# Half of a graph product with seven block products for eight, in a graph-attention kernel on one core

## The chip, the cores and the metric

The kernel runs on one core of one Trainium2 chip. Its time is the device time of one execution in microseconds. Each number from a trace comes from one profiled execution. Engines are named as the profile names them: PE (TensorE; PEld is its weight load), DVE (VectorE), ACT (ScalarE), POOL (GpSimd) and SP (SyncE, which here only issues transfers).

## The reference, cut to what matters

Two layers work on x of shape (16, 1024, 256): 16 images of 1024 nodes with 256 channels. The change lies in layer 0, in the product of the normed features with a weighted adjacency matrix.

```
h   = max(layernorm(x), 0)
fea = transpose(h, (0, 2, 1))                   # 256 channels x 1024 nodes
c   = mean over channels of fea                 # 1024 per image
A   = |  |sigmoid(c[m] - c[n]) - 0.5| - 0.5 | * 2, made symmetric
Wg  = adj * A                                   # 1024 x 1024 per image
g   = relu((fea @ Wg) * para)                   # the graph product
q   = g as queries, 4 heads of 64;  k, v = h @ kv_w
x   = x + softmax(q k^T * scale) v
# layer 1
h   = max(layernorm(x), 0)
x   = x + batchnorm(relu(batchnorm((A_hat @ h) @ W1^T + b1)) @ W2^T + b2)
```

## The kernel before

Everything is float32. The images run one after another, and the stages of neighbouring images are interleaved. The order of the instructions on PE, ACT, DVE, POOL and SP is the order in which the code records them (a manual schedule); every engine, and the queue of transfers that SP issues, works through its own list in that order. A wait arises where an instruction needs another engine's result, or a buffer that is still being read. Such buffers come from pools with a fixed number of places for each tag (`bufs`).

For image b the main loop records: `attention(b)`, then `graph(b+1)`, then `linear1_all(b)`, the first matmuls of layer 1. Work for image b+2 (norm, sums) is recorded inside linear1.

**graph(b)** multiplies h (8 chunks of 128 nodes, each 256 channels wide) with w (8 chunks of 128 x 1024, called `f_w`). For each chunk c there are four block products of 128x128 by 128x512: two halves of the channels (d) times two halves of the columns (g). They accumulate in two PSUM tiles `f_gps`, of two banks each. A chunk of w is made by `weights(b, c)`: Abs and Tanh on ACT, and on DVE the multiplication with the resident adjacency (the "mask", L350). The w tiles have five places (`w4`), so chunk c+5 is begun when chunk c has been used.

Between the chunks stand other steps (the dictionary `between`):

- `turn_h` turns h (DVE), and POOL issues 32 small transfers that place it as `f_hT` for keys and values.
- `left` holds what attention(b-1) left over: `[add0, collect, invert, spread, scale, add1]`. The attention output of an image comes in two halves g. For each half, `scale` multiplies by the reciprocal sums (L599) and issues 16 transfers on SP (L612) into the tile `f_att`; `add` adds that tile to the residual x (L620). `f_att` comes from the pool `ow` with one place. `add0` belongs to the first half, whose transfers were issued during attention; the other five belong to the second half.
- `norm` is the layer norm ahead of layer 1: `stats`, `invert` (a power on POOL), `shifts` and `relu` (eight activations on ACT).
- At chunk 5 SP loads `para` (two transfers of 512 KB, L387), and at chunk 6 the sums of key weights (`f_kt`, L393).

After the eight chunks, `queries` multiplies PSUM by `para` (L416, DVE) and applies Relu (L417, ACT). `values` makes v with two groups of products (`f_vps`, L424), each copied out by ACT (L431). The keys come from two halves by two blocks with seven products in place of eight (`mult`, L468; the copies on ACT are L478, L483, L488 and L493). One PSUM bank `f_kpsx` is added to several times there and copied out between the additions, so each addition waits for the copy before it. `f_vps`, `f_kpsx` and `f_gps` share three PSUM places of two banks with the score tiles of attention.

**linear1** starts with products of `norm.h` and the normalised adjacency (`f_aps`, L704). Inside it, the statistics of image b+2 run on DVE, and its relus on ACT ahead of the copy L756. Its x is loaded by SP (`arrive`, L189) into the place of the x that `leave` (L944) has just stored.

Of the kernel before, what the change touches and what calls it, by code (L numbers as in the profile page):

```python
# [29 lines left out]
def fast_path(  # L30
# [143 lines left out]
    with ExitStack() as stage:  # L174
# [115 lines left out]
        def prepare_start(b):  # L290

            sums_of[b] = small.tile([P, NC], F32, tag="sums", name=f"f_sums_{b}")
            norms[b] = Norm(xs[b], f"a{b}", sums_of[b])
            norms[b].stats(0, NC)
            norms[b].invert()
# [46 lines left out]
        def weights(b, c):  # L342


            w = w4.tile([P, N], F32, tag="w4", name=f"f_w_{b}_{c}")
            nc.scalar.activation(  # L346
                w, rows[b], AF.Abs, bias=cols[b][:, c : c + 1], scale=0.5 / C
            )
            nc.scalar.activation(w, w, AF.Tanh)  # L349
            nc.vector.scalar_tensor_tensor(w, w, 1.0, adj_t[c], ALU.subtract, ALU.mult)  # L350
            ws[b, c] = w

        hTs = {}

# [20 lines left out]
        def graph(b, between):  # L375


            gps = [ps_s.tile([P, N], F32, tag="s", name=f"f_gps_{b}_{d}") for d in range(CC)]
            hT = None
            para_t = []  # L380
            for c in range(NC):
                for step in between.get(c, ()):
                    step()
                if c == 5:
                    for d in range(CC):
                        t = w4.tile([P, N], F32, tag="w4", name=f"f_para_{b}_{d}")
                        nc.sync.dma_start(t, para_v[:, d, :])  # L387
                        para_t.append(t)
                if c == 6 and b > 1:
                    t23 = pp.tile([P, 2, 512], F32, tag="acc", name=f"f_kt23_{b}", bufs=2)  # L390
                    rest = pp.tile([P, 2, 512], F32, tag="acc", name=f"f_kt4_{b}", bufs=2)
                    sums = rest[:, 1].rearrange("p (n q) -> p n q", n=4)
                    nc.sync.dma_start(sums, kvs_d)  # L393
                w = ws.pop((b, c))
                blocks = [(d, g) for d in range(CC) for g in range(NH)]
                if b == 0 and c == 0:
                    blocks.sort(key=lambda n: n[1])
                for d, g in blocks:
                    nc.tensor.matmul(  # L399
                        gps[d][:, ts(g, 512)],  # L400
                        hs[b][:, c, ts(d, P)],
                        w[:, ts(g, 512)],
                        start=(c == 0),
                        stop=(c == NC - 1),
                    )
                if c == 0:
                    hT = hTs.pop(b)
            for step in between.get(NC, ()):
                step()
            kT = big.tile([P, CC, N], F32, tag="kT", name=f"f_kT_{b}")  # L410
            qT = big.tile([P, CC, N], F32, tag="qT", name=f"f_qT_{b}")
            v = big.tile([P, NC, C], F32, tag="v", name=f"f_v_{b}")

            def queries(d):

                nc.vector.tensor_mul(qT[:, d, :], gps[d], para_t[d])  # L416
                nc.scalar.activation(qT[:, d, :], qT[:, d, :], AF.Relu, scale=-SCALE)  # L417

            def values():
                for c4 in range(0, NC, 4):  # L420
                    ps = ps_s.tile([P, 4, C], F32, tag="s", name=f"f_vps_{b}_{c4}")
                    for i in range(4):
                        for e in range(CC):
                            nc.tensor.matmul(  # L424
                                ps[:, i, :],
                                hT[e][:, ts(c4 + i, P)],
                                kvw_t[:, e, C : 2 * C],
                                start=(e == 0),
                                stop=(e == CC - 1),
                            )  # L430
                    nc.scalar.copy(v[:, c4 : c4 + 4, :], ps)  # L431

            late = between.get("late", ())
            if b < 2:
                for step in late:
                    step()
                for d in range(CC):
                    ps = ps_s.tile([P, N], F32, tag="s", name=f"f_kps_{b}_{d}")
                    for g in range(NH):
                        for e in range(CC):  # L440
                            nc.tensor.matmul(  # L441
                                ps[:, ts(g, 512)],
                                kvw_t[:, e, ts(d, P)],
                                hT[e][:, ts(g, 512)],
                                start=(e == 0),
                                stop=(e == CC - 1),
                            )
                    nc.scalar.copy(kT[:, d, :], ps)
                    queries(d)
                values()  # L450
                return qT, kT, v

            t2, t3, t4 = t23[:, 0], t23[:, 1], rest[:, 0]
            part = lambda k, j: hT[k][:, ts(j, 512)]
            a = lambda i, k: kvw_t[:, k, ts(i, P)]
            for d in range(CC):
                queries(d)
            nc.vector.tensor_sub(t3, part(1, 1), part(0, 1))  # L460
            nc.vector.tensor_add(t2, t3, part(0, 0))
            nc.vector.tensor_sub(t4, part(1, 0), t2)
            values()
            t1 = part(0, 1)
            nc.vector.tensor_sub(t1, t1, part(0, 0))

            def mult(ps, left, right, more=False):
                nc.tensor.matmul(  # L468
                    ps, left, right, start=not more, stop=True, skip_group_check=more
                )  # L470

            c = lambda i, j: kT[:, i, ts(j, 512)]
            x = ps_s.tile([P, 512], F32, tag="s", name=f"f_kpsx_{b}")
            m7 = ps_s.tile([P, 512], F32, tag="s", name=f"f_kps7_{b}")
            m2 = ps_t.tile([P, 512], F32, tag="t", name=f"f_kps2_{b}")
            m4 = ps_o.tile([P, 512], F32, tag="o", name=f"f_kps4_{b}")
            mult(x, a(0, 0), part(0, 0))
            nc.scalar.copy(c(0, 0), x)  # L478
            mult(m2, a(0, 1), part(1, 0))
            nc.vector.tensor_add(c(0, 0), c(0, 0), m2)  # L480
            late[0]()
            mult(x, sums[:, 1], t2, True)
            nc.scalar.copy(c(1, 0), x)  # L483
            late[1]()
            mult(m7, sums[:, 2], t3)
            nc.vector.tensor_add(c(1, 0), c(1, 0), m7)
            mult(x, sums[:, 0], t1, True)
            nc.scalar.copy(c(1, 1), x)  # L488
            mult(m4, a(1, 1), t4)
            nc.vector.tensor_add(c(1, 1), c(1, 1), m7)  # L490
            nc.vector.tensor_add(c(1, 0), c(1, 0), m4)
            mult(x, sums[:, 3], part(1, 1), True)
            nc.scalar.copy(c(0, 1), x)  # L493
            return qT, kT, v

        def attention(b, qT, kT, v, hooks):

# [549 lines left out]
        with tc.manual_schedule(engines={ENG.PE, ENG.Activation, ENG.DVE, ENG.Pool, ENG.SP}):  # L1047
# [73 lines left out]
            for b in range(B):  # L1121
# [35 lines left out]
                if b + 1 < B:  # L1157
                    if 0 < b < B - 2:
                        thirds = load_thirds(b)
                    qkv = graph(b + 1, between)  # L1160
                    if b == 0:
                        for step in scale[4:]:
                            step()
                        thirds = make_thirds(b)
                if b + 2 < B:
# [1 line left out]
                        b,  # L1167
                        norm.h,
                        thirds,
                        lambda: prepare_start(b + 2),  # L1170
                        lambda: prepare_end(b + 2),
                        lambda: (prepare_row(b + 2), again(b + 1)),
                    )
# [55 lines left out]
    with ExitStack() as stage:  # L1229
# [21 lines left out]
        with tc.manual_schedule(engines={ENG.PE, ENG.Activation, ENG.DVE, ENG.Pool, ENG.SP}):  # L1251
# [40 lines left out]
            class Pair:  # L1292
# [49 lines left out]
                def m1(self):  # L1342
                    self.x = bank(f"f_zx_{self.p}", ps_x)
                    self.mult(self.x, a(0, 0), self.b[0, 0], True)

                def m2(self):
                    ps = bank(f"f_zm2_{self.p}")
                    self.mult(ps, a(0, 1), self.b[1, 0], True)
                    self.add(0, 0, ps)

                def m6(self):
                    self.mult(self.x, sums[:, 1], self.t2)
# [5 lines left out]
                def m5(self):  # L1358
                    self.mult(self.x, sums[:, 0], self.t1)

                def m3(self):
                    self.mult(self.x, sums[:, 3], self.b[1, 1])

                def m4(self):
                    self.mult(self.m, a(1, 1), self.t4)
# [20 lines left out]
            def plain(t, ps, f2):  # L1386
                for c in range(CC):
                    product(ps[c], t, c, f2)
# [717 lines left out]
```

## Time and profile before

| | |
|---|---|
| three runs | 2424.45, 2425.27, 2425.93 us; median 2425.27 |
| the profiled execution | 2425.91 us, of which 2424.1 are the span of the trace |
| mean granted TensorE clock | 0.995 |
| PE busy | 2384.8 us, 98% of the span |
| DVE, ACT, POOL busy | 1781.2, 1325.8 and 308.6 us |
| one image in the middle, graph product | 27.57 us (32 block products) |
| the same image, values and keys | 13.67 us |
| the same image, linear1 | 36.14 us |

The page gives busy time by engine, then the span in slices, the queues of transfers, the chain that ended last, and groups of instructions by line. A timeline line gives the start and the length in us, the engine, the line of the code, the operation, the tile written and the tiles read, the shape and the count; in square brackets stands how long the engine had idled before it, and what released it.

### The profile page before, as it was taken

To read this page: it belongs to the slowest core of one execution; us is meant where nothing else is said; L and a number is where in the kernel's file an instruction comes from. 1 tells how busy PE (TensorE), PEld (TensorE's weight loads), DVE (VectorE), ACT (ScalarE), POOL (GpSimd) and SP (SyncE) were. 2 spreads that over 40 slices of the span, in tenths; PEclk is the share of its full clock that TensorE was granted. 3 is DMA by queue.
4 is the path that set the end of the run, shared out by engine and by line. 5 is a ranking of instruction groups with operands and counts; after the bars stand their busy time and mean duration, and the time that the engine had idled before them with its cause. 6 is when DMAs were issued, how large, how long until landed. Compare 5 with 4: busy or idle time off the path is not lost.

```text
span 2424.1 us, 24651 instructions
## 1 busy us (share of the span) xinstructions
PE 2384.8 (98%) x8034; PEld 1050.7 (43%) x8034; DVE 1781.2 (73%) x2442; ACT 1325.8 (55%) x1932; POOL 308.6 (13%) x547
## 2 busy tenths in 40 slices
PE   8999999999999999999999999999999999999995
PEld 4453444434343434444343434344443434444444
DVE  6878778685959586786859595877868596757766
ACT  6845555464646455554646464555546465446654
POOL 2030202021020302020200203020202011000000
PEclk9999999999999999999999999999999999999998
DMA  5041414222332414142323324142423222355569
GB/s 187 9 140 61 152 61 126 87 88 74 115 95 62 146 61 152 61 126 87 89 73 115 95 63 146 61 152 61 126 87 88 73 68 85 101 192 195 176 239 375
DMA packets 176633, 275.76 MB, mean 114 GB/s; under 512 B 37872, under 2 KB 121328, under 8 KB 176496
## 3 DMA queue, kind: packets, MB, share of 16 engines
q1 hardware_dynamic: 156336, 241.55, 30.7%
q0 software_dynamic: 15552, 15.77, 2.5%
q10 hardware_dynamic: 4608, 16.78, 1.7%
q8 instruction: 66, 1.08, 0.2%
q14 instruction: 71, 0.58, 0.1%
HBM read 169.35 MB, written 71.10 MB: 99 GB/s over the span
## 4 chain that ended last, share of the span: by engine, by line
PE 93%; DVE 3%; DMA 2%; issue 1%; SPq 1%; POOL 0%; ACT 0%; DVEq 0%; ACTq 0%; POOLq 0%
PE f_s L507 17%; PE f_o L548 17%; PE f_gps L399 17%; PE f_aps L704 16%; PE f_zps L810 6%; PE f_vps L424 4%; PE f_zx L1326 4%; PE f_zm L1326 3%; PE f_kpsx L468 2%; PE f_kps L468 1%; DVE f_acc L524 1%; PE f_outps L1546 1%; PE f_z2ps L1264 1%; PE f_kps L441 1%; PE f_zps L892 1%
## 5 line engine op out<-in xcount | busy, mean ns | idle before, releaser
L515 ACT ACTIVATE f_p<-f_s 128x1024 f32<-128x1024 f32 x512 | 477.3, 1046 | 151.8 <-PE f_s L507 151.7
L524 DVE TENSOR_TENSOR f_acc<-f_acc,f_p 128x1024 f32<-128x1024 f32 x384 | 470.5, 1225 | 41.1 <-ACT f_p L515 0.5
L507 PE MATMUL f_s<-f_qT,f_kT 64*128 64x512 f32 x2048 | 456.8, 596 | 0.0
L548 PE MATMUL f_o<-f_p,f_v 128*64 128x512 f32 x2048 | 453.6, 595 | 0.0
L399 PE MATMUL f_gps<-f_w,f_h_a 128*128 128x512 f32 x1024 | 444.7, 594 | 0.3 <-DVE f_w L337 0.3
L369 POOL DMA_DIRECT2D f_hT<-f_hQ x480 | 235.9, 499 | 1221.7 <-PE f_gps L399 1170.8
L507 PEld LDWEIGHTS f_s<-f_qT,f_kT 64*128 64x128 f32 x2048 | 190.7, 185 | 263.6 <-ACT f_p L515 117.1
L399 PEld LDWEIGHTS f_gps<-f_w,f_h_a 128*128 128x128 f32 x1024 | 192.8, 190 | 247.0 <-issue 230.0
L548 PEld LDWEIGHTS f_o<-f_p,f_v 128*64 128x64 f32 x2048 | 141.4, 137 | 304.3 <-issue 254.2
L350 DVE SCALAR_TENSOR_TENSOR f_w<-f_w,f_adj 128x1024 f32<-128x1024 f32 x127 | 153.8, 1212 | 39.1 <-ACT f_w L349 39.1
L346 ACT ACTIVATE f_w<-f_row,f_col 128x1024 f32<-128x1024 f32 x127 | 147.0, 1157 | 29.3 <-DMA f_row<-frow 28.5
L279 ACT ACTIVATE f_h_b<-f_x,f_shift_b,f_rstd_b 128x256 f32<-128x256 f32 x128 | 67.9, 594 | 162.5 <-DVE f_shift_b L264 162.5
L349 ACT ACTIVATE f_w<-f_w 128x1024 f32<-128x1024 f32 x127 | 134.3, 1057 | 4.0
L704 PE MATMUL f_aps<-f_ahatT,f_hs 128*128 128x512 f32 x256 | 115.1, 592 | 0.0
L424 PE MATMUL f_vps<-f_kvw,f_hT 128*128 128x256 f32 x512 | 113.4, 379 | 0.2 <-DVE f_qT L416 0.2
L704 PE MATMUL f_aps<-f_ahatT,f_h_b 128*128 128x512 f32 x256 | 112.7, 593 | 0.0
L704 PE MATMUL f_aps<-f_t,f_hs 128*128 128x512 f32 x256 | 112.5, 592 | 0.0
L279 ACT ACTIVATE f_h_a<-f_x,f_shift_a,f_rstd_a 128x256 f32<-128x256 f32 x126 | 73.8, 587 | 62.6 <-DVE f_shift_a L264 62.6
L424 PEld LDWEIGHTS f_vps<-f_kvw,f_hT 128*128 128x128 f32 x512 | 97.2, 190 | 20.6 <-issue 7.4
L521 DVE TENSOR_TENSOR f_acc<-f_p,f_p 128x1024 f32<-128x1024 f32 x64 | 76.2, 1191 | 15.3 <-ACT f_p L515 15.3
L590 ACT COPY f_recs<-f_rec 32x32 f32<-32x32 f32 x128 | 31.5, 246 | 98.7 <-DVE f_rec L582 97.5
L575 ACT COPY f_parts<-f_red 32x64 f32<-32x64 f32 x128 | 39.0, 305 | 78.5 <-DVE f_red L540 77.3
(230 smaller groups left out, 2705.7 us busy)
## 6 DMA issues: line engine op xcount, KB each, us to landing
f_t<-ft SPq DMA_DIRECT2D x84, 512.0 KB, 6.9
fz<-f_z SPq DMA_DIRECT2D x64, 512.0 KB, 9.9
f_x<-in_x_dram SPq DMA_DIRECT2D x31, 1024.0 KB, 5.9
f_zb<-fz SPq DMA_DIRECT2D x42, 512.0 KB, 4.2
f_para<-in_L_gnn_para_dram SPq DMA_DIRECT2D x32, 512.0 KB, 4.5
f_att<-f_oT SPq DMA_DIRECT2D x512, 32.0 KB, 1.9
fx<-f_x SPq DMA_DIRECT2D x16, 1024.0 KB, 6.5
f_hT<-f_hQ POOLq DMA_DIRECT2D x480, 32.0 KB, 2.6
```

The costliest lines, as they stand in the source:

```text
L346: nc.scalar.activation(w, rows[b], AF.Abs, bias=cols[b][:, c : c + 1], scale=0.5 / C)
L350: nc.vector.scalar_tensor_tensor(w, w, 1.0, adj_t[c], ALU.subtract, ALU.mult)
L369: queue.dma_start(to[ts(k, 32), ts(a, 32 * NC)], t[ts(a, 32), k].rearrange("i c r -> i (c r)"),)
L399: nc.tensor.matmul(gps[d][:, ts(g, 512)], hs[b][:, c, ts(d, P)], w[:, ts(g, 512)], start=(c == 0), stop=(c == NC - 1),)
L424: nc.tensor.matmul(ps[:, i, :], hT[e][:, ts(c4 + i, P)], kvw_t[:, e, C : 2 * C], start=(e == 0), stop=(e == CC - 1),)
L507: nc.tensor.matmul(ps[:, e, :], kT[rows_e, pair, ts(m, P)], qT[rows_e, pair, ts(g, 512)], start=True, stop=True,)
L515: nc.scalar.activation(p, ps, AF.Exp)
L524: nc.vector.tensor_add(acc_of[s], acc_of[s], p)
L548: nc.tensor.matmul(o_of[s][e * HD : (e + 1) * HD, :], v[:, m, ts(2 * pair + e, HD)], p[:, e, :], start=(m == 0), stop=(m == NC - 1),)
L704: nc.tensor.matmul(ps, left[:, m, :], right(m), start=not more and m == 0, stop=(m == KH - 1), skip_group_check=more,)
L810: nc.tensor.matmul(ps[i], left[:, ts(i, P)], right, start=not more, stop=True, skip_group_check=more,)
L1326: nc.tensor.matmul(ps, left[:, m, :], right[:, m, :], start=start and m == 0, stop=(m == 1), skip_group_check=not start,)
```

## The change

Images 2 to 15 take a new function `graph_seven`; images 0 and 1 keep `graph`. In it:

- Chunks 0 to 3 are multiplied as before (`plain`). Chunks 4 to 7 form two pairs, (4, 5) and (6, 7). Each pair is a product of two by two blocks with two by two blocks, done with seven block products. All pairs add into the same banks: the two `f_gps` tiles, one bank x and one bank m7.
- That needs sums of h (`s1` to `s4`, 128x256 each) and differences of w (`t1` to `t4`, 128x512 for each pair), all on DVE. `t1` and `t4` are made in place. `t2` and `t3` lie in the tile that later holds the keys.
- x is copied out three times on ACT, into the tile that later holds the values (`room`). DVE then adds m7 and the `f_gps` banks to it, and multiplies the sum by `para`. `para` is loaded in one transfer of 1 MB into the tile of the queries (`f_qT`) and multiplied in place.
- `add0` is recorded behind the seven-product part; `collect`, `invert`, `spread` and `scale` stay between the first chunks; `add1` goes to the keys. The statistics of the norm go behind the queries and into the keys; its relus, the query relus, `leave` and `arrive` are recorded between or behind the key products.

```diff
         def weights(b, c):
+            differences(b, c)
+            masked(b, c)
+
+        def differences(b, c):
             w = w4.tile([P, N], F32, tag="w4", name=f"f_w_{b}_{c}")
...
+            gps = [ps_s.tile([P, N], F32, tag="s", name=f"f_gps_{b}_{d}") for d in range(CC)]
+            add0, collect, invert, spread, scale, add1 = left
...
+            turn_h(b)
+            differences(b, 2)
+            masked(b, 2)
+            collect()
+            invert()
+            differences(b, 3)
+            masked(b, 3)
+            differences(b, 4)
+            spread()
+            scale()
+            masked(b, 4)
+            plain(0)
+            differences(b, 5)
+            masked(b, 5)
...
+            nc.vector.tensor_sub(s3, a(0, 0), a(1, 0))
+            nc.vector.tensor_add(s1, a(1, 0), a(1, 1))
+            nc.vector.tensor_sub(s2, s1, a(0, 0))
+            nc.vector.tensor_sub(s4, a(0, 1), s2)
+            plain(1)
+            differences(b, 6)
+            masked(b, 6)
...
+            make_t3(0)
+            make_t1(0)
+            plain(2)
+            differences(b, 7)
+            masked(b, 7)
+            make_t2(0)
+            plain(3)
+            qT = big.tile([P, CC, N], F32, tag="qT", name=f"f_qT_{b}")
+            nc.sync.dma_start(qT, para_v)
...
+            nc.sync.dma_start(sums, kvs_d)
+            make_t3(1)
+            make_t1(1)
+            make_t2(1)
...
+            m1(0)
+            m2(0)
+            m1(1)
+            nc.scalar.copy(room[:, 0], x)
+            m_7(0)
+            m3(0)
+            m2(1)
+            make_t4(0)
+            make_t4(1)
+            m6(0)
+            m_7(1)
+            m3(1)
+            m6(1)
+            nc.scalar.copy(room[:, 2], x)
+            m4(0)
+            m4(1)
+            m5(0)
+            m5(1)
+            nc.scalar.copy(room[:, 1], x)
+            add0()
+            nc.vector.tensor_add(room[:, 2], room[:, 2], m7)
...
+            nc.vector.tensor_sub(kt3, part(1, 1), part(0, 1))
+            nc.vector.tensor_add(kt2, kt3, part(0, 0))
+            nc.vector.tensor_sub(kt4, part(1, 0), kt2)
+            nc.vector.tensor_add(room[:, 3], room[:, 1], m7)
+            both = lambda d: room[:, 2 * d : 2 * d + 2].rearrange("p n k -> p (n k)")
+            for d in range(CC):
+                nc.vector.tensor_add(both(d), both(d), gps[d])
+            for d in range(CC):
+                nc.vector.tensor_mul(qT[:, d, :], both(d), qT[:, d, :])
...
+            norm.stats(0, 4)
+            norm.invert(0, 4)
+            values(b, hT, v)
...
+            mult(x, aw(0, 0), part(0, 0))
             nc.scalar.copy(c(0, 0), x)
+            mult(k2, aw(0, 1), part(1, 0))
+            nc.vector.tensor_add(c(0, 0), c(0, 0), k2)
+            norm.shifts(0, 4)
+            add1()
+            norm.stats(4, NC)
+            norm.invert(4, NC)
+            leave(b - 1)
+            arrive(b + 1)
+            mult(x, sums[:, 1], kt2, True)
             nc.scalar.copy(c(1, 0), x)
+            behind[0](todo)
...
             nc.scalar.copy(c(1, 1), x)
+            behind[1](todo)
...
             nc.scalar.copy(c(0, 1), x)
+            behind[2](todo)
+            return (qT, kT, v), todo
```

For images 2 to 14 `behind` holds the norm's relus (two chunks, two chunks, four chunks), and the query relus follow in linear1. For image 15 it holds the two query relus and then all eight relus of the norm.

## The prediction

> **What bounds the kernel now.** I read the page's busy line first, then the TensorE timeline of one image in the middle of the run, and then the other engines' timelines over the same stretch.
>
> ```profile
> PE 2384.8 (98%) x8034; PEld 1050.7 (43%) x8034; DVE 1781.2 (73%) x2442; ACT 1325.8 (55%) x1932; POOL 308.6 (13%) x547
> ```
>
> TensorE has 39 us of 2424 free, most of it at the two ends. So removed TensorE work pays in full, and any new stall costs in full. The timeline of image 8 (start and length in us):
>
> ```profile
> 1055.47 27.73 PE L399 MATMUL f_gps<-f_w,f_h_a 128*128 128x512 f32 x64
> 1083.04 3.62 PE L424 MATMUL f_vps<-f_kvw,f_hT 128*128 128x256 f32 x16
> 1086.83 3.72 PE L424 MATMUL f_vps<-f_kvw,f_hT 128*128 128x256 f32 x16 [0.17 <-DVE f_qT L416]
> ...
> 1092.14 1.12 PE L468 MATMUL f_kpsx<-f_kt,f_kt 128*128 128x512 f32 x2
> ...
> 1096.71 7.03 PE L704 MATMUL f_aps<-f_ahatT,f_h_b 128*128 128x512 f32 x16
> ```
>
> Each product of 128x128 by 128x512 is two records. The row's mean of 594 ns is a latency: 64 records fill 1083.04 - 1055.47 = 27.57 us, so one product costs 27.57 / 32 = **0.86 us**. Below, times count from the graph product's start, T = 1055.47. The third key product (`f_kpsx` from `f_kt`) starts at T+36.7, linear1 at T+41.2.
>
> VectorE and SyncE in that stretch:
>
> ```profile
> 1061.18 1.21 DVE L620 TENSOR_TENSOR f_x<-f_x,f_att 128x1024 f32<-128x1024 f32 x1
> ...
> 1064.73 1.21 DVE L599 TENSOR_TENSOR f_oT<-f_oT,f_recs 128x1024 f32<-128x1024 f32 x1
> ```
>
> ```profile
> 1065.96 10.18 SPq L612 DMA_DIRECT2D f_att<-f_oT  x16
> 1076.24 1.00 SPq L387 DMA_DIRECT2D f_para<-in_L_gnn_para_dram  x2
> 1077.55 0.33 SPq L393 DMA_DIRECT2D f_kt<-fkvs  x1
> ```
>
> L620 is the first half's residual add (left[0]); it is the last reader of the only `att` buffer (pool `ow`, bufs=1). It ends before L599 (scale), so the second half's 16 transfers into that buffer start as L599 ends. SyncE spends 10.2 us issuing them, 0.64 each, and only then issues `para` and the key sums, early enough for L416 at T+30.
>
> **What the Trainium skill says.** "DMA: Bandwidth & Descriptors", section "Anatomy of one DMA — SWDGE (gpsimd) path": any semaphore wait happens on the issuing sequencer before dispatch; the DMA engines don't wait. The lines above agree (L612 begins 0.02 us after L599's end): a held transfer holds the queue behind it. "VectorE: DVE Perf Modes", section "The TRN2 errata — SBUF-src ops pay a fixed extra latency per instruction": an fp32 tensor_tensor takes (N+151)/0.96 ns. The page's 690 ns at 512 and 1225 at 1024 agree; 128x256, which this trace lacks, is then an estimated 0.42 us. "TensorE: Matmul & The Clock Gate", section "Part 1: The HAM clock gate (the "warmup" mystery)": after an idle window of about 3.4 us the array runs at half clock until a busy window has passed. The kernel's tail agrees, in the timeline and in the windows (columns: window, length, busy PE, PEld, DVE, ACT, POOL, granted clock, DMA share, GB/s):
>
> ```profile
> 2386.90 6.36 PE L1546 MATMUL f_outps<-f_ident,f_z 128*128 128x128 f32 x32 [5.37 <-ACT f_z L1526]
> 2393.69 2.13 PE L1546 MATMUL f_outps<-f_ident,f_z 128*128 128x128 f32 x16 [0.44 <-DVE f_x1t L1587]
> ```
>
> ```profile
> 2385.00:2390.00 5.00, 3.08 (x13) 2.69 (x14) 0.82 (x1) 3.61 (x3) 0.00 (x0) 0.51 1.02 368
> 2390.00:2395.00 5.00, 4.56 (x30) 3.96 (x30) 4.30 (x5) 3.62 (x3) 0.00 (x0) 0.81 1.03 420
> ```
>
> After 5.4 us idle the clock is 0.51, and a 5 us window at mean 0.81 was at half clock for 1.9 us: the gate opened some 5 us after the restart, 2 to 2.5 us of work lost.
>
> **The change, part by part** (images 2 to 15, 14 in all).
>
> TensorE: chunks 4 to 7 take 14 products instead of 16: -2 x 0.86 = -1.72 us an image, -24 us in all. The graph product ends at T+25.8 if its operands are in time.
>
> VectorE operands: `w2`'s mask ends its slot at T+5.7 as before. Then collect's reduction, reciprocal, most and least (1.28), `w3` mask (1.14 start to start): 8.1. Scale waits for spread, which ScalarE reaches after `w4` (7.5, +1.02): it runs 8.5 to 9.6. Masks of `w4` and `w5`: 11.9. Four 128x256 sums of h (0.34 to 0.46 start to start): 13.5. `w6` mask 14.65, t3 and t1 of pair 0: 16.0, `w7` mask 17.1, then six 128x512 differences at 0.60 to 0.72: 21.0. TensorE wants `w7` at T+18, the last t at T+23: **hidden**. If that cover were gone, all 11 us that VectorE gains an image (4 x 0.42 + 10 x 0.69 + 2 x 1.22) would be at stake.
>
> The three ScalarE copies of x (0.59 each) lie behind other products: nothing. The adds of both halves and room before the queries would let the second value product begin at T+30.1, where TensorE arrives at 29.2: 0.9 us, absorbed in what follows.
>
> **add0 moves** behind all of this, to T+21.0, ending at 22.2. Scale's 16 transfers stay ahead of it, but write the one `att` buffer that add0 still has to read. The first must wait for add0: it starts at T+22.2 instead of 10.5. Queued behind on SyncE are 15 more transfers, `para` (now one of 1 MB, into qT), the key sums, the store of x and the load of x of b+2. So:
>
> - 16 issues at 0.64: `para` is issued at T+32.4.
> - It lands 5.4 us later, at 37.8. Bounds: 3.8 (the smallest `f_para`) to 6.5. Two 512 KB ones took 4.5 each, half a us apart; 1 MB of x takes 5.9:
>
> ```profile
> f_x<-in_x_dram SPq DMA_DIRECT2D x31, 1024.0 KB, 5.9
> f_para<-in_L_gnn_para_dram SPq DMA_DIRECT2D x32, 512.0 KB, 4.5
> fx<-f_x SPq DMA_DIRECT2D x16, 1024.0 KB, 6.5
> ```
>
> - The two query multiplications: 1.14 + 1.22, to 40.15.
> - v serves as room that they read, so ScalarE's copies of the value products wait for them: the second is done at 41.2. The first key copy is queued behind: 41.75.
> - The third key product adds into the bank that this copy reads: T+41.8 instead of 36.7, **+5.1 us**.
>
> TensorE has by then been idle from 35.2, 6.6 us: cold clock. Five us at half rate, of which ScalarE's copies between key products hide a little: **+2.3 us** (0 to 3.5). Linear1 starts at T+48.6.
>
> Later norm: add1, stats and inversion (44.6 to 47), shifts and the eight relus of 0.55 fit ahead of linear1's needs chunk by chunk: nothing. The store of x issues at 44.6 instead of 23.8 and lands after 6.5; the next load then takes 5.9, to 57. Linear1's VectorE wants x at 7.7 us after its start, 56.3: 0.7 late, covered by the slack ahead of L753 (2.8 us idle). If it takes longer, up to 1.5 us lands on the product that waits for L756's copy. The query relus move into linear1, where ScalarE idles 6.3 us: nothing.
>
> Image 15: no linear1 follows; eight relus (4.3 us) stand ahead of the first exponentials, and score tiles have three buffers (2.65 us of TensorE work): +3.4 us.
>
> Sum: 14 x (5.1 + 2.3) + 3.4 = 107 us; the 1.72 saved are already inside, since both times are absolute. The profiled execution took 2425.9 us (span 2424.1 and 1.8 around it), so 2533; the median is 0.6 lower: **2532 us**.
>
> **The rivals.**
> 1. *TensorE's saving decides.* If the transfers were not held (another buffer, or a wait met early), the third key product could start when VectorE's additions allow, about T+35.3 against 36.7: -1.4 x 14 = -20 us, 2405; at best -24, 2401. For it: the product's operands are in time. Against: one `att` buffer. It decides only if `para` lands before about T+32.5, where issue alone takes until 32.4.
> 2. *The late queue also breaks linear1.* The load of x for b+2 slips further and the norm for the next image delays L756's copy: +1.5 us an image, `para` at 6.5 and the cold clock for a second window (+1.2 each): 14 x (7.4 + 3.9) + 3.4 = +162, 2587. For it: nothing on SyncE is late now, but a dozen transfers become so. Against: 2.8 us of slack at L753.
> 3. *The delay without the clock*: the gate stays open and `para` takes 3.8: 14 x 3.5 + 3.4 = +52, 2477. Against: 6.6 us of idle against the tail's 5.4.
>
> **How the numbers follow.** Forecast 0.75, rival 2 0.13, rival 3 0.09, rival 1 0.03. The range 2488 to 2575 holds the first with its bounds and about half of rivals 2 and 3. About 0.2% (5 us) is what a measurement can tell from no change; only rival 1 is faster: 0.03, within it 0.01, slower 0.96.
>
> **What would show it.** In the changed profile the second `f_att` group should begin only when the first `f_x<-f_x,f_att` add of the image ends; `f_kpsx` should wait about 6.6 us on ScalarE's `f_kT` 14 times; the granted clock should sink to about half for some 5 us in each keys stage; DVE busy should be near 1935 us, PE records 56 fewer. It is wrong if `para` is issued before T+28, if the keys stage has no gap, or if the wait stands in the graph product itself (VectorE late), where I put none.

## The result: slower by 4.3%, and the profile after

The changed kernel takes 2529.28 us (median; 2527.63 to 2531.64) against 2425.6 for the kernel before beside it: ratio 1.0428, 95% interval 1.041 to 1.0447. The forecast was 2532. The profiled spans are 2525.8 and 2424.1, so there are 101.7 us to account for. One run each of two kernels further down took 4190 and 9855 us; it counts in the median there, but not in the ratio. Times written T+ count, as in the prediction, from the start of an image's graph product.

The page of the changed kernel, the line of busy times:

```profile
PE 2387.9 (95%) x7978; PEld 1050.9 (42%) x7978; DVE 1926.7 (76%) x2694; ACT 1348.1 (53%) x1974; POOL 318.1 (13%) x561
```

The removed products are gone (7978 records against 8034) and VectorE has gained 145 us, yet TensorE's share fell: the span grew, not the work. The list of TensorE's waits names one place (what waited, for what: us in total, times, longest):

```profile
PE f_kpsx L625 <- ACT f_kT L641: 92.3, 14, 7.7
```

TensorE's timeline of image 8, T = 1101.20 (start, length in us, idle before):

```profile
1101.20 14.00 PE L469 MATMUL f_gps<-f_w,f_h_a 128*128 128x512 f32 x32
...
1127.06 3.62 PE L444 MATMUL f_vps<-f_kvw,f_hT 128*128 128x256 f32 x16
1131.94 3.72 PE L444 MATMUL f_vps<-f_kvw,f_hT 128*128 128x256 f32 x16 [1.27 <-DVE f_v L610]
...
1142.98 2.07 PE L625 MATMUL f_kpsx<-f_kt,f_kt 128*128 128x512 f32 x2 [5.60 <-ACT f_kT L641]
1144.85 1.51 PE L625 MATMUL f_kps<-f_kt,f_kt 128*128 128x512 f32 x2
...
1148.85 7.03 PE L875 MATMUL f_aps<-f_ahatT,f_h_b 128*128 128x512 f32 x16
```

The graph product ends at T+25.9 without a gap inside, 1.7 us earlier than before. The third key product starts at T+41.8, and the pair takes 2.07 us where 1.12 was seen before. What TensorE waits for is found by going back through SyncE, VectorE and ScalarE over the same stretch:

```profile
1122.98 10.50 SPq L783 DMA_DIRECT2D f_att<-f_oT  x16
1133.53 0.59 SPq L537 DMA_DIRECT2D f_qT<-in_L_gnn_para_dram  x1
1134.43 0.32 SPq L542 DMA_DIRECT2D f_kt<-fkvs  x1
```

```profile
1121.73 1.22 DVE L791 TENSOR_TENSOR f_x<-f_x,f_att 128x1024 f32<-128x1024 f32 x1
...
1138.98 2.36 DVE L612 TENSOR_TENSOR f_qT<-f_v,f_qT 128x1024 f32<-128x1024 f32 x2 [5.96 <-DMA f_qT<-in_L_gnn_para_dram]
```

```profile
1140.31 2.13 ACT L451 COPY f_v<-f_vps 128x1024 f32<-128x1024 f32 x2 [12.47 <-DVE f_qT L612]
1142.34 0.59 ACT L641 COPY f_kT<-f_kpsx 128x512 f32<-128x512 f32 x1
```

SyncE's 16 transfers begin 0.03 us after add0 (L791) ends; `para` issues at T+32.3, VectorE gets it at T+37.8, the value copies and the first key copy follow in ScalarE's order. The copies of the value products (L451) stand behind the query multiplications because those still read the tile that becomes v. That is the chain of the prediction, link by link.

The means over images 2 to 14, from the timelines, give the sum ("to linear1" is the time from the start of the third key product to that of linear1, "one image" from one graph product to the next):

| | third key product | to linear1 | linear1 starts | one image |
|---|---|---|---|---|
| before | T+36.26 | 4.56 | T+40.83 | 133.31 |
| after | T+41.61 | 6.33 | T+47.94 | 140.43 |

13 images times 7.12 are 92.6 us; image 15 and what follows it grew by 9.65 (6.66 ahead of its scores, 2.99 behind their start); everything ahead of image 2 shrank by 0.5. Together that is the 101.7, to rounding.

### The profile page after: what moved, and what is told of

It is laid out like the page before. It is cut to its first block, busy times and chain, and to the rows that moved or that the text cites. A ratio compares the mean times of both kernels' runs of the same rounds, so it can differ in the third digit from the quotient of the medians.

```text
span 2525.8 us, 24862 instructions
## 1 busy us (share of the span) xinstructions
PE 2387.9 (95%) x7978; PEld 1050.9 (42%) x7978; DVE 1926.7 (76%) x2694; ACT 1348.1 (53%) x1974; POOL 318.1 (13%) x561
## 4 chain that ended last, share of the span: by engine, by line
PE 69%; DVE 11%; ACT 7%; SPq 5%; DMA 4%; issue 3%; DVEq 0%; ACTq 0%; POOLq 0%; POOL 0%
PE f_aps L875 15%; PE f_s L678 15%; PE f_o L719 14%; PE f_zps L981 6%; SPq L783 5%; PE f_zx L1522 4%; DMA f_qT<-in_L_gnn_para_dram 3%; PE f_zm L1522 3%; ACT f_p L686 3%; DVE f_w L358 2%; DVE f_acc L695 2%; PE f_kpsx L625 2%; PE f_gps L401 2%; PE f_kps L625 1%; DVE f_qT L612 1%
## 5 line engine op out<-in xcount | busy, mean ns | idle before, releaser
L469 PE MATMUL f_gps<-f_w,f_h_a 128*128 128x512 f32 x448 | 196.0, 595 | 0.0
L469 PEld LDWEIGHTS f_gps<-f_w,f_h_a 128*128 128x128 f32 x448 | 84.0, 190 | 111.8 <-issue 98.1
L451 ACT COPY f_v<-f_vps 128x1024 f32<-128x1024 f32 x32 | 32.4, 1012 | 181.4 <-DVE f_qT L612 172.2
L444 PE MATMUL f_vps<-f_kvw,f_hT 128*128 128x256 f32 x512 | 113.9, 380 | 4.3 <-DVE f_v L610 4.3
L625 PE MATMUL f_kpsx<-f_kt,f_kt 128*128 128x512 f32 x28 | 28.9, 1134 | 92.3 <-ACT f_kT L641 92.3
L612 DVE TENSOR_TENSOR f_qT<-f_v,f_qT 128x1024 f32<-128x1024 f32 x28 | 33.1, 1222 | 102.4 <-DMA f_qT<-in_L_gnn_para_dram 102.4
L444 PEld LDWEIGHTS f_vps<-f_kvw,f_hT 128*128 128x128 f32 x512 | 97.1, 190 | 25.4 <-issue 7.4
L279 ACT ACTIVATE f_h_a<-f_x,f_shift_a,f_rstd_a 128x256 f32<-128x256 f32 x126 | 73.8, 587 | 37.8 <-DVE f_shift_a L264 37.8
```

The source lines that it names most:

```text
L444: nc.tensor.matmul(ps[:, i, :], hT[e][:, ts(c4 + i, P)], kvw_t[:, e, C : 2 * C], start=(e == 0), stop=(e == CC - 1),)
L469: nc.tensor.matmul(gps[d][:, ts(g, 512)], h[:, c, ts(d, P)], w[:, ts(g, 512)], start=(c == 0), stop=(c == PLAIN - 1),)
```

## Experiments

**First round: the delay, its parts, its price.** Four kernels take the delay apart, each by one change to the changed kernel; a fifth makes a delay of the same kind without the new product. Two more look at the clock and at image 15. (A line that an experiment inserts moves the numbers behind it by one.)

*The early add.*

```
             differences(b, 2)
             masked(b, 2)
+            add0()
             collect()
...
             nc.scalar.copy(room[:, 1], x)
-            add0()
```

> The changed kernel with one step moved back: the first half's residual add (add0) stands behind w2's mask again, ahead of collect, everything else as changed. Queue theory (the late add holds the only att place, so 16 transfers and para behind them are late): para issues at about T+20.6 and lands by T+26, the third key product starts at T+34.5 (TensorE's own arrival), linear1 at T+39.1 against 47.9 in the changed kernel and 40.8 before; 14 images save 1.7 us each and image 15 still loses about 3, so about 2404 us, faster than before. If w7's mask, now 1.2 us later with 0.2 us to spare, becomes late: up to 1 us more an image, 2418. VectorE rival (the 18 added VectorE instructions or the room that holds v are what makes the queries late): the third key product stays near T+41 and the time within 10 us of the changed kernel's, 2520 to 2535.

Measured: 2451.61 us, ratio 1.011 (1.0093 to 1.0127): 78 us better than the changed kernel, but slower than before. Both theories missed. SyncE did what was expected, with `para` issued at T+20.7 in image 8 (T = 1063.98):

```profile
1074.11 10.49 SPq L783 DMA_DIRECT2D f_att<-f_oT  x16
1084.64 0.59 SPq L538 DMA_DIRECT2D f_qT<-in_L_gnn_para_dram  x1
```

The wait for the key copy is gone from TensorE's list, and a smaller one has its place, one product earlier:

```profile
PE f_vps L444 <- DVE f_v L610: 28.9, 13, 3.4
```

The second value product waits for VectorE's adds into room. VectorE's timeline of image 8 tells why:

```profile
1087.22 0.69 DVE L601 TENSOR_TENSOR f_v<-f_v,f_gps 128x512 f32<-128x512 f32 x1 [1.82 <-ACT f_v L595]
1092.63 0.69 DVE L604 TENSOR_TENSOR f_kt<-f_hT,f_hT 128x512 f32<-128x512 f32 x1 [4.72 <-DMA f_hT<-f_hQ]
...
1095.48 2.35 DVE L610 TENSOR_TENSOR f_v<-f_v,f_gps 128x1024 f32<-128x1024 f32 x2
```

L604 is the first of three sums for the key products. It stands between the two halves of the room adds and reads the last transposed pieces of h, which GpSimd's 32 small transfers bring. It waits for them; L610, which needs none of this, waits behind it. Over all images that wait is 9.9 us (5 times) in the changed kernel and here

```profile
  DMA f_hT<-f_hQ: 47.5, 13
```

(what the idle time ahead of that line ended with: us in total, times). L604 starts at T+24.7 on average in the changed kernel (images 2 to 15) and at T+27.3 here, although GpSimd ends issuing at T+22.9 and T+23.1. So the pieces land later here, where att and `para` move beside them; in the changed kernel the late add kept both back, and the wait hardly showed. Which of the two matters is taken up in the second round.

*Another place for att, the add left late.* The second half's att goes into the place of the sums, and the graph product's sums of h into an idle place; no engine's or queue's order changes.

```
-        t = ow.tile([P, HEADS // 2, 4, 4, 32], F32, tag="att", ...)
+        t = ow.tile([P, HEADS // 2, 4, 4, 32], F32, tag=("att", "sums")[g], ...)
...
-            sums_h = ow.tile([P, 4, 2, P], F32, tag="sums", ...)
+            sums_h = ow.tile([P, 4, 2, P], F32, tag="oT", ..., bufs=2)
```

> The changed kernel with add0 left late, but the second half's att takes another place (that of the sums, whose graph-product use moves into the free oT place): order of every engine and queue is the same, only the wait for add0 is gone. Queue theory: the 16 transfers start when scale ends (T+9.5), para issues near T+20, third key product at T+34.5, about 2404 us, as with the early add within 5 us. Theory that the place of add0 in VectorE's order costs by itself (rival): no better than half of the gain, 2460 or more.

Measured: 2452.06 us, 1.0115 (1.0096 to 1.0134). `para` issues at T+20.0 as expected, and the time equals that of the early add. So the add's place costs nothing by itself; the one place of att turned it into 77 us. The absolute number missed for the reason just given (31.2 us of the same wait at L444).

*`para` ahead of the transfers, the add left late.*

```
+            qT = big.tile([P, CC, N], F32, tag="qT", ...)
+            nc.sync.dma_start(qT, para_v)
             turn_h(b)
             differences(b, 2)
...
-            qT = big.tile([P, CC, N], F32, tag="qT", ...)
-            nc.sync.dma_start(qT, para_v)
```

> The changed kernel with para's load issued at the head of the stage, ahead of the 16 att transfers; add0 stays late. Queue theory: para is there by about T+10, the query multiplications follow the adds into room at T+29.6 to 32; what is left late is the load of the key sums, still behind the 16 held transfers: issued at T+32.4, landing 3 to 5 us later, at T+35.4 to 37.4, so the third key product starts there, not at 41.6, and waits for that load. About 1 to 3 us an image over the early add, little or no cold clock: 2418 to 2450 us. If add0 itself or add1 (its 16 transfers still land at T+34) sets the time by the later norm: linear1 still near T+47 and 2510 or more.

Measured: 2429.36 us, 1.0013 (1.0005 to 1.002). Of the held queue, `para` is what mattered: with it out, 100 of the 104 us are gone while the 16 transfers and add1 stay late. The reason given for the rest was wrong. The third key product (T+36.7) follows the first by 1.8 us, TensorE's own pace, so the late key sums hold nothing; 16.1 us are lost at L444, behind the wait for the transposed h.

*Half of the transfers on GpSimd's queue.*

```
-                            nc.sync.dma_start(
+                            queue = nc.gpsimd if half and a % 2 else nc.sync
+                            queue.dma_start(
...
-            scale()
+            scale(True)
```

> The changed kernel with 8 of the second half's 16 att transfers issued by GpSimd's queue instead of SyncE's; add0 late, one att place. Queue theory with 0.64 us for each issue: para issues 8 x 0.64 = 5.1 us earlier, near T+27.2, and lands near T+32.4; multiplications to 34.8, copies of v to 35.9, key copy to 36.5: third key product at T+36.6 instead of 41.6, 2 us after TensorE gets there, clock not cold: 5 + 1.5 us an image less, about 2435 us (2425 to 2455). If the wait itself and not the number of issues sets the delay: third key product still at T+41 and 2520 or more.

Measured: 2439.78 us, 1.0062 (1.0045 to 1.0079), third key product at T+36.4 (13 images). SyncE, image 8 (T = 1056.96):

```profile
1079.08 5.09 SPq L784 DMA_DIRECT2D f_att<-f_oT  x8
1084.21 0.59 SPq L537 DMA_DIRECT2D f_qT<-in_L_gnn_para_dram  x1
```

Eight issues take 5.09 us, `para` goes at T+27.25, and the start moves by 5.2 us. The delay is a wait for add0 plus a count of issues. The Trainium skill, "DMA: Bandwidth & Descriptors", section "Issuing engines are not separate DMA queues", says that spreading transfers over issuing engines saves only the sequencer's time to initiate them, usually small beside the transfer. Here it isn't small: 0.64 us each, in a row, ahead of a load that is waited for.

*The delay without the new product.* The kernel before, with left[0] and its statistics behind w7's mask:

```
     0: [
-        lambda: turn_h(b + 1), more(2), left[0], left[1], left[2], more(3),
+        lambda: turn_h(b + 1), more(2), left[1], left[2], more(3),
...
-    2: [more(6), lambda: norm.stats(0, 4)],
+    2: [more(6)],
...
-    4: [left[5], lambda: norm.stats(4, NC), norm.invert],
+    4: [left[0], lambda: norm.stats(0, 4), left[5], lambda: norm.stats(4, NC), norm.invert],
```

> The kernel before with its 16 block products, but the first half's add and its statistics moved behind w7's mask, ahead of the second half's add: the delay alone, without the new product. Queue theory: att transfers start at T+17.7, two loads of para issue at T+28 and land at T+33; VectorE's multiplications stand behind the second add (T+30), its statistics and the shift, so they start near T+37; the second value product waits for the first of them, at about T+38 instead of 31; with a cold clock 8 to 10 us an image, 2535 to 2570 us. Rival (only together with the new product is the late add harmful): within 10 us of 2425.

Measured: 2545.65 us, 1.0488 (1.0471 to 1.0506). TensorE waits at its second value product:

```profile
PE f_vps L424 <- DVE f_qT L416: 75.0, 14, 5.9
```

The last link is another one than in the changed kernel, as expected. The two loads of `para` land by T+33.8 in image 8 (T = 1115.66), and the multiplications start only at T+35.3, with no wait for them: VectorE has waited for the late att at the second add, and the statistics stand behind that.

```profile
1145.87 1.22 DVE L620 TENSOR_TENSOR f_x<-f_x,f_att 128x1024 f32<-128x1024 f32 x1 [10.09 <-DMA f_att<-f_oT]
...
1150.95 2.35 DVE L416 TENSOR_TENSOR f_qT<-f_gps,f_para 128x1024 f32<-128x1024 f32 x2
```

With the early add and the late one, in the old order and the new, there are four kernels: 2425.6 and 2545.7 old, 2451.6 and 2529.3 new. The late add costs 120 us in the old order and 78 in the new one, so a held att queue is costly without the new product too. The two costs are not the same quantity: in the old order the statistics moved along with the add, and image 1 is delayed as well. The delay isn't the whole of the change either: with the early add the changed kernel still loses 26.

*TensorE kept busy in the gap.* Six products whose result is overwritten:

```
             nc.vector.tensor_add(c(0, 0), c(0, 0), k2)
+            for _ in range(6):
+                mult(k4, aw(0, 0), part(0, 0))
             norm.shifts(0, 4)
```

> The changed kernel with six unused 128x128x512 products put between the second and the third key product (their result is overwritten): TensorE works through 5.2 of the 6.6 us gap. Clock theory: the third key product still starts near T+41.6, but the last key products run at full rate; from there to linear1 4.6 us instead of 6.3, so 1.5 us an image less (1.2 to 2.3): 2500 to 2512 us. If the clock costs nothing (rival R3): 2529 within 4. If TensorE's own work lies in the way: slower than 2530.

Measured: 2511.18 us, 1.0347 (1.0329 to 1.0364), 18.1 us less with more work. The windows (window, length, busy PE, PEld, DVE, ACT, POOL, granted clock, DMA share, GB/s) of image 8, in the changed kernel and then here:

```profile
1137.00:1142.00 5.00, 0.38 (x1) 0.00 (x0) 3.02 (x5) 1.58 (x2) 0.00 (x0) 1.00 0.35 142
1142.00:1147.00 5.00, 4.02 (x6) 1.78 (x7) 4.46 (x15) 2.50 (x5) 1.34 (x1) 0.66 0.00 0
1147.00:1152.00 5.00, 5.00 (x13) 2.15 (x12) 3.33 (x12) 4.13 (x8) 1.01 (x1) 1.00 0.63 213
```

```profile
1131.00:1136.00 5.00, 4.56 (x11) 1.65 (x10) 4.46 (x15) 3.66 (x7) 1.34 (x1) 1.00 0.00 0
```

The first key product behind the gap starts as late as before (T+41.69), but from there to linear1 it is 4.55 us instead of 6.33: the clock's share is 1.78 us an image. Of these 13 x 1.78 = 23 us, linear1 takes back 3 (0.24 an image: 24.27 against 24.03 from its start to the first `f_zps`), the key product itself 1, image 15 and what follows it 2, and the part ahead of image 2 another 1. That leaves the 15.9 us by which the two profiled spans differ (2525.8 and 2509.9); the medians differ by 18.1.

*Image 15.* The early add, and the eight relus of image 14's later norm spread over image 15's attention, two behind each of its four groups of scores:

```
-                                lambda todo: norm.relu(0, NC, False),
+                                lambda todo: None,
...
+                    for i in range(4):
+                        hooks.setdefault(i, []).append(
+                            lambda i=i: kept.relu(2 * i, 2 * i + 2, False))
```

> The early add, and the eight relus of image 14's second norm moved from ahead of image 15's scores into its attention, two behind each group of scores. If the eight relus are what image 15 loses (2.7 us of waiting by the scores for ScalarE in the changed kernel): 2.5 to 3 us less than with the early add alone, about 2401 us; ratio to before 0.990. If they only move the wait elsewhere: the same as the early add alone, 2404.

Measured: 2461.62 us, 1.0133 (1.0115 to 1.015): slower than the early add. Linear1 does start 3.3 us sooner after T than there, and then stops:

```profile
PE f_aps L875 <- DVE f_hs L860: 8.2, 1, 8.2
```

SyncE's waits and timeline show the same fault that the change has, in another place (T = 2016.67):

```profile
SPq L189 <- ACT f_h_b L279: 62.9, 15, 49.0
...
2107.79 0.38 SPq L189 DMA_DIRECT2D f_x<-in_x_dram  x1
2108.23 0.57 SPq L1304 DMA_DIRECT2D f_w2n<-in_L_gnn_W_dram  x1
2108.96 12.96 SPq L783 DMA_DIRECT2D f_att<-f_oT  x16
```

The reload of x (L189) overwrites the tile that the relus read. With the last relu ending at T+91, the reload is held until then, and image 15's own transfers behind it; its residual add, and behind that the sums of h for linear1, are late. In the profiles this kernel is 12.7 us longer than that of the early add; 5.2 of them lie ahead of image 15, where the edit changes nothing and the wait at L444 happens to be longer (32.8 us in all, against 28.9).

**Second round: what is left once the transfers are early.**

*The three sums behind the queries*, on top of the early add:

```
-            nc.vector.tensor_sub(kt3, part(1, 1), part(0, 1))
-            nc.vector.tensor_add(kt2, kt3, part(0, 0))
-            nc.vector.tensor_sub(kt4, part(1, 0), kt2)
             nc.vector.tensor_add(room[:, 3], room[:, 1], m7)
...
                 nc.vector.tensor_mul(qT[:, d, :], both(d), qT[:, d, :])
+            nc.vector.tensor_sub(kt3, part(1, 1), part(0, 1))
+            nc.vector.tensor_add(kt2, kt3, part(0, 0))
+            nc.vector.tensor_sub(kt4, part(1, 0), kt2)
```

> The early add (as before), and VectorE's three sums of hT for the key products (kt3, kt2, kt4) moved from between the two pairs of room adds to behind the query multiplications. New theory: with the early add, the three sums wait for the last transposed transfers of h (47.5 us in 13 images), and the adds into room, which the second value product needs, stand behind them on VectorE. Moved: room adds end at T+29.7, the second value product starts at T+29.3 to 29.9 with almost no wait, multiplications end at 32.0, the sums at 34.2, copies of v at 34.3, key copy at 34.9, third key product at T+35.0, linear1 at 39.6: 1.2 us an image less than before, image 15 about 3 more: about 2412 us (2404 to 2422). If the second value product itself waits for the transposed h: 2430 or more.

Measured: 2422.22 us, 0.9986 (0.998 to 0.9993). The wait at L444 is gone and the third key product starts at T+34.53: all 1.73 us of the removed products have arrived there. That settles the cause of the loss with the early add. But linear1 starts at T+40.25, 5.72 us later, where 4.56 is usual.

*The same sums moved, the add left late*:

> The changed kernel with add0 late, and only the three sums moved behind the query multiplications. Both theories expect little: para lands at T+37.8 whatever stands in VectorE's order, and now the sums come after the multiplications: kt2 at T+41.6, no later than the key copy; 2525 to 2535 us. It shows that the wait for the transposed h costs something only once the transfers of att are early.

Measured: 2536.88 us, 1.046 (1.0445 to 1.0475), third key product at T+41.46. No gain, as expected; the 7.6 us above the changed kernel are more than expected. In the profile 5 of them lie between the third key product and linear1 (6.71 us, against 6.33); their cause was not followed up.

*Relus of image 14 all at the first hook* (`hooks[0] = [lambda: kept.relu(0, NC, False)]`), on top of the moved sums:

> The same, and the eight relus of image 14's second norm all behind the first group of scores of image 15 (not spread over four groups, where they held the reload of x on SyncE's queue and image 15's transfers behind it until T+91). Expected: ScalarE does them while TensorE multiplies the first values, the reload of x issues near T+52, nothing later is held: 2.5 to 3 us less than with them ahead of the scores, about 2409 us. Rival (they are never free): no less.

Measured: 2418.81 us, 0.9971 (0.9961 to 0.9982), 3.4 less than without: the eight relus were image 15's loss, and early in the attention they are free. The absolute number missed by 10, as that of the moved sums had.

*And `para` first*:

> The same as the last, and para's load at the head of the stage, so that its 1 MB does not move beside the last transposed transfers of h. If para's bytes are what makes those late: the second value product waits less, 3 to 8 us less in all than with para behind att. If it is the 16 small att transfers that run beside them: no difference, within 3 us.

Measured: 2420.01 us, 0.9977 (0.9968 to 0.9987): 1.2 us more than without, within the 3 that were expected for no difference. VectorE no longer waits for the transposed h in either kernel, so the time can't tell what makes it late, but the landing of its last piece in the traces (means of images 2 to 14) tells part of it. It lands at T+24.3 in the changed kernel, at T+26.3 with `para` alone early, at T+27.3 with the early add, at T+27.2 in the last kernel and at T+26.9 here. So `para` alone makes it 2.0 us later, and taking `para` out of the way of the early att gains only 0.3. How the traffic does it stays open.

*The relus one place back.* In the kernel with 2418.81 us, ScalarE of image 8 (T = 1052.64) shows where 1.16 us go between the third key product and linear1, and TensorE the wait:

```profile
1090.30 1.09 ACT L279 ACTIVATE f_h_b<-f_x,f_shift_b,f_rstd_b 128x256 f32<-128x256 f32 x2 [1.40 <-DVE f_shift_b L264]
1091.30 0.56 ACT L656 COPY f_kT<-f_kpsx 128x512 f32<-128x512 f32 x1
```

```profile
1091.92 1.12 PE L625 MATMUL f_kpsx<-f_hT,f_kt 128*128 128x512 f32 x2 [0.64 <-ACT f_kT L656]
```

Two relus of the later norm wait for its shift, with a key copy behind them.

```
-                                lambda todo: norm.relu(0, 2, False),
-                                lambda todo: norm.relu(2, 4, False),
-                                lambda todo: norm.relu(4, NC, False),
+                                lambda todo: None,
+                                lambda todo: norm.relu(0, 2, False),
+                                lambda todo: norm.relu(2, NC, False),
```

> The fastest so far (early add, sums behind the queries, image 14's relus at the first hook), and in images 2 to 14 the first two relus of the later norm moved one place back on ScalarE, behind the second of the three remaining key copies instead of ahead of it. In that kernel the copy stands behind two relus (1.09 us), and these behind the norm's shift (T+37.5): the last key product waits 0.64 us for it, and linear1 starts at T+40.24, 5.72 us after the third key product, where 4.56 is the least seen. Theory (ScalarE's order is what the later norm costs): linear1 at T+39.1, 1.1 us less in 13 images, 14 us: about 2405 us, ratio 0.991. Rival: the relus are then late for linear1's first chunks, and the wait goes there: no less, within 3 us of 2419.

Measured: 2419.2 us, 0.9973 (0.9963 to 0.9984): the rival is right that nothing is gained, but not on where. Linear1 starts at T+39.43, 0.8 us earlier, and gives it back inside. TensorE's wait is shown first, then ScalarE, VectorE and SyncE of image 8 (T = 1054.63):

```profile
PE f_aps L875 <- ACT f_u L927: 8.9, 13, 1.3
```

```profile
1115.46 0.56 ACT L927 COPY f_u<-f_aps 128x512 f32<-128x512 f32 x1
```

```profile
1105.31 2.71 DVE L251 BATCH_NORM_STATS2 f_st_a<-f_x 128x6 f32<-128x256 f32 x8 [3.11 <-DMA f_x<-in_x_dram]
```

```profile
1093.65 0.37 SPq L1115 DMA_DIRECT2D fx<-f_x  x1
1099.81 0.38 SPq L189 DMA_DIRECT2D f_x<-in_x_dram  x1
```

The load of x lands at T+50.7. Statistics, shift and eight relus of the next norm follow, and L927 stands behind them. The load was issued at T+45.2, since it overwrites the tile of the store of x, and that could only go at T+39.0, when the second residual add was done; in the kernel before, store and load went at T+23.8 and T+39.4 (image 8). So it is the later norm that now takes the products' saving, first through ScalarE's order and then through the store and load of x: 0.50 us an image of 1.73 are left in the fastest kernel (132.81 against 133.31).

## Why the prediction was right, point by point

- **TensorE's saving** (-1.72 an image): right. The graph product ends at T+25.85, and the records are 56 fewer. VectorE's operands are hidden: no product of the seven waits. VectorE busy 1926.7, forecast 1935. One reading was wrong without effect: the trace of before does have additions of 128x256 (L1287 takes 419 ns), and they agree with the 0.42 us that I took for missing.
- **add0, the one att place, 16 issues, `para`**: right to within half a microsecond. Transfers from T+21.8 (forecast 22.2), `para` issued at 32.3 (32.4), there at 37.8 (37.8), third key product at 41.8 (41.8) in image 8. The early add and the three experiments that bring `para` forward by place, by order and by count show the cause. The late add in the kernel before shows that a held att queue costs without the new product as well, though there the second add, and not `para`, is what comes last. The term of +5.1 is 5.35 over 13 images: I measured against image 8 of before, which is late itself (36.67, where the mean is 36.26).
- **Cold clock** (+2.3): right in kind, too large; 1.77 to 1.78 measured. I took the tail's restart, "some 5 us" at half rate. In the trace the clock is at half for 3.41 us (images 4, 8 and 12), 6.83 (nine images) or 10.24 (images 2 and 5), and part of that falls into the gap, where it costs nothing. Behind the start of the third key product it is 2.8 to 6.0 us, 3.8 on average; half of that is 1.89, and that 0.12 less is lost fits the forecast that ScalarE's copies hide a little. Image 2, with T = 255.35 and the third key product at 296.8, is one of the longest:

```profile
297.50:302.50 5.00, 5.00 (x7) 2.00 (x6) 4.46 (x14) 1.73 (x4) 1.44 (x2) 0.50 0.32 107
```

The Trainium skill, "TensorE: Matmul & The Clock Gate", section "Part 1: The HAM clock gate (the "warmup" mystery)", gives a window of 3413 ns, and the three lengths are one, two and three of it. Half rate for one window would lose an estimated 1.71. That this is near the mean is chance: single images lose 1.3 to 2.8.

- **Image 15** (+3.4): 3.0 measured after its scores start, and moving the relus gained 3.4.
- **Later norm (the one ahead of layer 1): nothing**: right for this kernel only. From its start to the first `f_zps` linear1 took 24.03 us before and after, as the load of x stayed covered. The cover was the delay itself: without it the later norm takes 1.2 us an image of the saving.
- **Sum**: 14 x (5.35 + 1.77) + 3.0 - 0.5 would be 102; 101.7 measured. Two terms that are off by +0.25 and -0.5 an image partly cancel, which is luck.
- **Rival 1** (transfers not held: 2401 to 2405) was rightly given little chance, but its price was wrong by 47 us. It took the third key product to start at T+35.3 as soon as `para` is early. I had named the wait for VectorE's adds at L610, yet not the wait for transposed h that stands ahead of them on VectorE. Once the sums are moved it is reached (T+34.53), and the later norm still keeps it from 2405.
- **Rival 2** (linear1 breaks too) did not happen: the same 24.03 us in both. **Rival 3** (no clock) is refuted by the kept-busy run.

## What to carry to other kernels

When a step is moved, ask first what place it releases and which queue holds a transfer into that place: one in-order queue turned a 1.2 us add into 78 us, and my own experiment repeated it with eight relus and a reload of x. Price the counterfactual as carefully as the forecast: a delay covers other lateness (here the transposed h, then relus, then a load), and each cover has to be taken off in turn before removed work becomes time. When several sums can follow each other on an in-order engine, put the one whose operands come last behind those that somebody waits for.

## What the hardware showed that I had not expected

A much shorter gap than 6.6 us can cost the clock. In the early-add run the second value product waits 2 us or more in nine images. Two of them are images 4 and 14, in TensorE's timeline:

```profile
558.46 3.72 PE L444 MATMUL f_vps<-f_kvw,f_hT 128*128 128x256 f32 x16 [2.77 <-DVE f_v L610]
...
1907.43 5.41 PE L444 MATMUL f_vps<-f_kvw,f_hT 128*128 128x256 f32 x16 [2.01 <-DVE f_v L610]
```

After 2.77 us idle nothing is lost; after 2.01 us the same 16 matmuls take 1.69 us longer. Of the nine, four lost 1.69 us (the clock was at half for 3.41 us), two about 3.0 (at half for 6.83 us; idle 3.01 and 3.30), and three nothing. The sum, 4 x 1.69 + 2 x 3.0 = 12.7 us, is part of what the early add loses. With another place for att, image 6 paid after only 1.85 us idle.

What decides is where the gap lies. In each of the fourteen traces all switches of the granted clock fall on a grid of 3.413 us, to 0.001 us. These are its intervals around the two gaps, in the columns of the windows above: two that share image 4's gap and the one behind them, then the one that holds image 14's gap and the one behind it:

```profile
553.24:556.66 3.42, 2.44 (x12) 1.80 (x10) 2.26 (x4) 0.00 (x0) 0.00 (x0) 1.00 0.01 2
556.66:560.07 3.41, 1.61 (x7) 1.44 (x8) 3.31 (x4) 0.00 (x0) 0.00 (x0) 1.00 0.00 0
560.07:563.48 3.41, 3.41 (x14) 2.28 (x12) 3.38 (x11) 2.28 (x3) 0.00 (x0) 1.00 0.00 0
...
1904.92:1908.33 3.41, 1.40 (x7) 0.92 (x6) 3.31 (x4) 0.00 (x0) 0.00 (x0) 1.00 0.00 0
1908.33:1911.75 3.42, 3.42 (x10) 2.72 (x9) 3.42 (x7) 1.01 (x1) 0.00 (x0) 0.50 0.02 5
```

The longer gap is split by a point of the grid into 0.98 and 1.80 us, and the clock stays full; the shorter one lies in one interval, and the clock is at half in the next. Counted over all fourteen traces from 120 us on, an interval at full clock with under 1.8 us of TensorE idle was followed by full clock each time (9249 intervals), one with 2.2 us or more by half clock each time (96), and of the 35 between 23 were followed by half clock. From half clock back to full, under 0.5 us idle was enough each time (101), and with 1.0 us or more it never came back (78). The Trainium skill, "TensorE: Matmul & The Clock Gate", section "Part 1: The HAM clock gate (the "warmup" mystery)", puts the idle window at about 3.4 us and calls it free-running. The grid agrees with that; but here a window that was idle for little more than half was enough.
